# Fewer, larger transfers on the SP queue of a two-layer graph network kernel

## The chip, the core and the metric

The kernel runs on one core of a Trainium2 chip. The core has five engines that run side by side: TensorE (PE in the profile; its weight loads are listed apart as PEld), VectorE (DVE), ScalarE (ACT), GpSimd (POOL) and SyncE (SP). Each takes its own instructions in order and waits on semaphores for the others. Data moves between the chip's memory (HBM, here also called DRAM) and the on-chip memory by 16 DMA engines, which SP, ACT and GpSimd feed with transfers through queues. The metric is the time of one execution on the device, in microseconds (us); before the change it is 1118.38 us, the median of 3 runs (1115.33 to 1119.31).

## What is computed

The inputs are x of shape (32, 512, 512), an adjacency matrix adj of (512, 512), and weights of 512 x 512, all float32. Two layers follow each other, each with a normalisation ahead of it and a residual sum behind it:

```python
# layer 0
h = maximum(layernorm(x), 0)
x = x + (einsum('nm,bmd->bnd', adj, h) @ weight + bias)
# layer 1
h = maximum(layernorm(x), 0)
q, k, v = h @ Wq + bq, h @ Wk + bk, h @ Wv + bv        # 8 heads of 64
scores = einsum(q, k) / sqrt(64) + (1 - adj) * -1e9
x = x + (softmax(scores) @ v) @ Wo + bo
```

With these inputs the mask of layer 1 is decided in each row by its largest entry of adj, so that a softmax row picks one row of v. The kernel looks at adj at run time, and if this holds for every row it takes a shorter path (`single_path`): layer 1 becomes "take row idx(n) of h, multiply it by Wv Wo, add a constant row, and add the product to row n of x". That is the path that runs here.

## The kernel before

**Tiles.** A batch of x is one tile of 128 partitions x 4 row blocks x 512 columns (1 MB). Five such buffers are kept (`xs`, batch b uses buffer b % 5), and two for the normalised rows (`hs`).

**The work of a batch.** Normalise x (DVE statistics L194 and L195, a power on POOL L201, an offset on DVE L204, the activation on ACT L212); multiply by adj (`aggregate`, copied from PSUM to yT by ACT L326 and DVE L324); multiply by the layer-0 weight and add onto x (`layer0`, DVE L344); normalise again (L194 to L212, result h1). Then layer 1: `put_h` stores h1 to a DRAM tile hs (L488); `get_h` gathers from it, with eleven indirect DMAs issued by POOL (L494), only the rows that some row of adj picks, at most 352; DVE transposes them (L529); `layer1` multiplies them by the folded weight (ACT L337 and DVE L334 take the results to zs); `put_z` transposes the products back on DVE in two parts (L545, tile zr) and writes them to a DRAM tile z by SP (L549); `finish` has four indirect DMAs issued by POOL gather, for each of the 512 rows, its row of z and add it onto x (L553); `store` writes x to the output by SP (L559).

**Matrix products.** All three products of a batch are done by a scheme with seven block products in place of eight (`product`, L287). It accumulates several of them in one PSUM bank, and between two of them the bank has to be read: `u2` goes into the bank of `p1` after p1 was taken, `c22` after u2 was taken, `c12` after p5 was taken. So PE waits when DVE (layer 0) or ACT (aggregate) takes a block late.

**Order.** Nothing is scheduled by a planner: under `tc.manual_schedule()` each engine runs its instructions in the order in which they are written. An outer loop runs over b, and its 21 steps are PE's block products of `layer0(b)`, `aggregate(b + 1)` and `layer1(b - 1)`. `put(batch, step, f)` hangs other work on a step: in a usual turn, z of batch b - 2 at step 0 (the blocks s = 0 to 5), `finish(b - 2)` at step 1, the load of x for b + 2 at step 2, the power of h1 at steps 6 and 8, `put_h(b)` at steps 9 and 11, `store(b - 2)` at step 12, and the first part of z of batch b - 1 (the blocks s = 6 to 10) at step 20. The last two turns differ: z of batch 29 has steps 13 and 14, its additions step 15, and its store goes behind those of the loop. At the very end `layer1_rows(31)` does the last batch row by row, with its own four stores, and the store of batch 30 is issued from ACT's queue.

**The SP queue** holds the loads of x, the stores of h1, z and the output, in that order of steps. [...]

Of the kernel before, what the change touches and what calls it, by code (L numbers as in the profile page):

```python
# [17 lines left out]
P = 128  # L18
# [8 lines left out]
def gnn_two_layers(ctx: ExitStack, tc: tile.TileContext, x, adj, w0, b0, wq, bq, wk, bk, wv, bv, wo, bo, out):  # L27
# [149 lines left out]
    with tc.If(single > P - 1) as cmp:  # L177
        single_path(tc, x, wv, bv, wo, bo, out, kept)
# [38 lines left out]
def single_path(ctx: ExitStack, tc: tile.TileContext, x, wv, bv, wo, bo, out, kept):  # L217
# [14 lines left out]
    nc = tc.nc  # L232
    B, N, D = x.shape
    C, DC = N // P, D // P
# [12 lines left out]
    X, H0 = {0: xs[0], 1: xs[1]}, {0: hs[0], 1: hs[1]}  # L247
    H0S, H1, HS, HC, HT, HTS, Z, ZT, ZR = {}, {}, {}, {}, {}, {}, {}, {}, {}

    def load_x(b):  # L250
        X[b] = xs[b % 5]
        for c in range(C):
            nc.sync.dma_start(X[b][:, c, :], x[b, c * P:(c + 1) * P, :])


    def blk(t, chunks, cols, half=HALF):
# [284 lines left out]
    def put_z(b, s0, s1):  # L541
        if b not in Z:
            Z[b] = dram.tile([32 * S, D], F32, name="z")
            ZR[b] = work.tile([P, S, P], F32, name="zr")
        nc.vector.transpose(ZR[b][:, s0:s1, :].rearrange("p s (c e) -> p s c e", c=4),  # L545
                            ZT[b][:, :, 32 * s0:32 * s1].rearrange("p c (s j) -> p s c j", j=32))
        rows = Z[b].rearrange("(s j) (q f) -> q j s f", j=32, q=4)
        for q in range(4):
            nc.sync.dma_start(rows[q][:, s0:s1, :], ZR[b][32 * q:32 * q + 32, s0:s1, :])  # L549

    def finish(b):
        for c in range(C):
# [1 line left out]
                out=X[b][:, c, :], out_offset=None, in_=Z[b],  # L554
                in_offset=bass.IndirectOffsetOnAxis(ap=place[:, c:c + 1], axis=0), compute_op=ALU.add)

    def store(b, eng=nc.sync):
        for c in range(C):
            eng.dma_start(out[b, c * P:(c + 1) * P, :], X[b][:, c, :])  # L559

    def run(steps, work_by_step):
        if steps is None:
# [16 lines left out]
    with tc.manual_schedule():  # L579
# [6 lines left out]
        for b in range(B + 1):  # L586
# [5 lines left out]

            put(b - 2, 15 if b == B - 1 else 1, finish)
            put(b + 2, 2, load_x)
            for step, i in ((0, 0), (1, 1), (2, 2), (3, 3)) if b > 0 else ((1, 0), (2, 1), (2, 2), (3, 3)):
                put(b + 1, step, h0_sum, i)
            put(b - 2, 14 if b == B - 1 else 0, put_z, 0, 6)
            if b == B - 1:
                put(b - 2, 13, put_z, 6, S)
# [22 lines left out]
            if b < B - 1:  # L622
                put(b - 2, 12, store)
            elif b == B:
                put(b - 3, 1, store)
# [13 lines left out]
            if b < B and b != B - 2:  # L639
                put(b - 1, 20, put_z, 6, S)  # L640
# [36 lines left out]
                run(layer1(b - 1) if b < B and b != B - 2 else None, todo[14:21])  # L677
        layer1_rows(B - 1)
        if B > 1:
            store(B - 2, nc.scalar)  # L680


@with_exitstack
# [261 lines left out]
```

## Time and profile before

| | before |
|---|---|
| timed, median of 3 (lowest to highest) | 1118.38 us (1115.33 to 1119.31) |
| profiled execution | 1170.05 us, span 1168.3 us |
| mean granted TensorE clock | 0.984 |
| busy: DVE, POOL, ACT | 905.7, 653.9, 359.4 us |
| moved by DMA | 186.90 MB, mean 160 GB/s |
| SP issues: x loads L253, stores L559, z L549 | 120, 120, 248 |

Busy time is the time in which an engine executes; a DMA issue is not busy time. The profiled execution is some 50 us longer than the timed ones. The page's list of transfers shows what SP issues (name out<-in, engine, operation, count, size of one):

```profile
hs<-h SPq DMA_DIRECT2D x64, 512.0 KB
out_dram<-x SPq DMA_DIRECT2D x124, 256.0 KB
x<-in_x_dram SPq DMA_DIRECT2D x120, 256.0 KB
z<-zr SPq DMA_DIRECT2D x124, 96.0 KB
z<-zr SPq DMA_DIRECT2D x124, 80.0 KB
```

The three kinds that the change touches are the last four rows (four of the 124 output stores belong to the last batch and stay). A batch has 4 + 4 + 8 of them, beside two stores of h1.

### The profile page before, as it was taken

To read this page: it belongs to the slowest core of one execution; us is meant where nothing else is said; L and a number is where in the kernel's file an instruction comes from. 1 tells how busy PE (TensorE), PEld (TensorE's weight loads), DVE (VectorE), ACT (ScalarE), POOL (GpSimd) and SP (SyncE) were. 2 spreads that over 40 slices of the span, in tenths; PEclk is the share of its full clock that TensorE was granted. 3 is DMA by queue.
4 is the path that set the end of the run, shared out by engine and by line. 5 is a ranking of instruction groups with operands and counts; after the bars stand their busy time and mean duration, and the time that the engine had idled before them with its cause. 6 is when DMAs were issued, how large, how long until landed. Compare 5 with 4: busy or idle time off the path is not lost.

```text
span 1168.3 us, 15855 instructions
## 1 busy us (share of the span) xinstructions
PE 1100.6 (94%) x5408; PEld 957.8 (82%) x5408; DVE 905.7 (78%) x1859; ACT 359.4 (31%) x655; POOL 653.9 (56%) x584
## 2 busy tenths in 40 slices
PE   7999989999989999999999999899999999999885
PEld 3658878989978989888989888798998889998782
DVE  6879868878867878787888888687887878887760
ACT  4223313233313233323323332223333232233120
POOL 2146536655646765565765555566565656666443
PEclk9999989999989999999999999999999999999998
DMA  6414665655666665576665657566566756666438
GB/s 225 153 19 129 165 173 140 171 170 149 168 173 139 165 180 147 153 191 167 150 177 171 159 155 187 133 170 178 155 165 172 190 140 167 180 176 156 120 118 203
DMA packets 135146, 186.90 MB, mean 160 GB/s; under 512 B 17472, under 2 KB 61120, under 8 KB 135056
## 3 DMA queue, kind: packets, MB, share of 16 engines
q1 hardware_dynamic: 102320, 123.05, 31.0%
q0 software_dynamic: 29472, 56.47, 27.4%
q10 hardware_dynamic: 3264, 6.29, 1.5%
q8 instruction: 44, 0.72, 0.2%
q14 instruction: 46, 0.38, 0.1%
HBM read 96.28 MB, written 89.46 MB: 159 GB/s over the span
## 4 chain that ended last, share of the span: by engine, by line
PE 83%; DVE 6%; issue 3%; POOL 3%; ACT 1%; DMA 1%; another core or an unknown queue 1%; SPq 0%; POOLq 0%; ACTq 0%; DVEq 0%
PE mm L287 78%; DVE x L344 2%; POOL x L553 1%; PE mm L139 1%; PE mm L480 1%; PE mm L371 1%; DVE st L194 1%; DMA x<-in_x_dram 1%; PE mm L520 1%; ACT h L212 1%; POOL rstd L201 1%; POOL hc L494 1%; DVE h0s L266 1%; DVE yT L324 0%
## 5 line engine op out<-in xcount | busy, mean ns | idle before, releaser
L494 POOL DMA_INDIRECT hc<-hs,listed x341 | 356.2, 1045 | 261.9 <-DMA hs<-h 157.2
L344 DVE TENSOR_TENSOR x<-mm,x 128x512 f32<-128x512 f32 x217 | 149.6, 690 | 146.6 <-PE mm L287 107.7
L326 ACT COPY yT<-mm 128x512 f32<-128x512 f32 x124 | 71.8, 579 | 614.3 <-PE mm L287 478.3
L553 POOL DMA_INDIRECT x<-z,place x124 | 196.0, 1581 | 70.2 <-issue 47.9
L287 PE MATMUL mm<-w_t,sel 128*128 128x256 f32 x744 | 182.2, 396 | 37.9 <-DVE x L344 31.6
L212 ACT ACTIVATE h<-x,off,rstd 128x512 f32<-128x512 f32 x256 | 194.7, 807 | 48.2 <-DVE off L204 46.3
L287 PEld LDWEIGHTS mm<-w_t,sel 128*128 128x128 f32 x744 | 143.9, 196 | 67.5 <-DVE x L344 39.4
L201 POOL TENSOR_TENSOR rstd<-ve,mhalf 128x2 f32<-128x2 f32 (+1 forms) x97 | 97.2, 1002 | 156.9 <-DVE ve L200 151.8
L194 DVE BATCH_NORM_STATS2 st<-x 128x6 f32<-128x512 f32 x256 | 171.6, 670 | 8.4 <-DMA x<-in_x_dram 7.3
L287 PE MATMUL mm<-adjT_s,h0s 128*128 128x256 f32 x744 | 170.9, 379 | 0.4 <-ACT yT L326 0.2
L287 PEld LDWEIGHTS mm<-adjT_s,h0s 128*128 128x128 f32 x744 | 141.2, 190 | 20.3 <-ACT yT L326 1.2
L287 PE MATMUL mm<-hTs,wvo_t 128*128 128x176 f32 x720 | 117.8, 313 | 1.7 <-ACT zs L337 1.7
L287 PE MATMUL mm<-w_s,yT 128*128 128x256 f32 x496 | 117.2, 379 | 0.0
L287 PE MATMUL mm<-adjT,h 128*128 128x256 f32 x496 | 117.2, 379 | 0.0
L337 ACT ACTIVATE zs<-mm,cvo_c 128x176 f32<-128x176 f32 x248 | 87.4, 404 | 94.7 <-PE mm L287 60.4
L287 PEld LDWEIGHTS mm<-hTs,wvo_t 128*128 128x128 f32 x720 | 109.7, 190 | 2.8 <-ACT zs L337 2.8
L287 PEld LDWEIGHTS mm<-adjT,h 128*128 128x128 f32 x496 | 94.2, 190 | 13.2 <-issue 0.5
L287 PEld LDWEIGHTS mm<-w_s,yT 128*128 128x128 f32 x496 | 93.1, 190 | 11.7 <-issue 0.5
L458 DVE TENSOR_TENSOR x<-x,b_r 128x512 f32<-128x512 f32 x128 | 86.5, 677 | 0.0
L287 PE MATMUL mm<-hT,wvo 128*128 128x176 f32 x480 | 81.4, 313 | 0.0
L287 PEld LDWEIGHTS mm<-hT,wvo 128*128 128x128 f32 x480 | 75.3, 190 | 1.5
L324 DVE TENSOR_TENSOR yT<-mm,yT 128x512 f32<-128x512 f32 x93 | 63.5, 682 | 4.1 <-PE mm L287 2.7
(152 smaller groups left out, 1262.9 us busy)
## 6 DMA issues: line engine op xcount, KB each, us to landing
hs<-h SPq DMA_DIRECT2D x64, 512.0 KB
out_dram<-x SPq DMA_DIRECT2D x124, 256.0 KB
x<-in_x_dram SPq DMA_DIRECT2D x120, 256.0 KB
z<-zr SPq DMA_DIRECT2D x124, 96.0 KB
z<-zr SPq DMA_DIRECT2D x124, 80.0 KB
hc<-hs,listed POOLq DMA_INDIRECT x341
x<-z,place POOLq DMA_INDIRECT x124
x<-in_x_dram ACTq DMA_DIRECT2D x4, 256.0 KB
```

Source lines behind the costliest of these rows:

```text
L139: nc.tensor.matmul(ps, hs[0][:, m, d * P:(d + 1) * P], adjT[:, m, :], start=(m == 0), stop=(m == C - 1))
L194: self.nc.vector.bn_stats(st, self.src[:, self.chunks[i], :])
L201: self.nc.gpsimd.tensor_tensor(self.rstd, ve, self.mhalf[:, 0:n], ALU.pow)
L212: self.nc.scalar.activation(dst, src, AF.Relu, bias=self.off[:, i:i + 1], scale=self.rstd[:, i:i + 1])
L287: nc.tensor.matmul(bank[:, m, 0:half], lhs[:, k, m * P:(m + 1) * P], rhs[:, k, :], start=(first and m == 0 and k == 0), stop=(k == 1), ski ...
L324: nc.vector.tensor_add(dst, bank, dst)
L326: nc.scalar.copy(dst, bank)
L337: nc.scalar.activation(dst[:, m, :], bank[:, m, :], AF.Identity, bias=cvo_c[:, 2 * i + m:2 * i + m + 1])
L344: nc.vector.tensor_add(dst, bank, dst)
L458: nc.vector.tensor_add(X[b][:, c, :], X[b][:, c, :], b0_r)
L494: nc.gpsimd.indirect_dma_start(out=HC[b][:, s, :], out_offset=None, in_=HS[b].rearrange("n (q d) -> (n q) d", q=4), in_offset=bass.Indirec ...
L553: nc.gpsimd.indirect_dma_start(out=X[b][:, c, :], out_offset=None, in_=Z[b], in_offset=bass.IndirectOffsetOnAxis(ap=place[:, c:c + 1], axi ...
```

## The change

The transfers of a batch are merged: x is loaded by one DMA of 1 MB in place of four of 256 KB, the output is stored by one of 1 MB in place of four, and z is written by four of 176 KB, after the second transpose, in place of four of 80 KB after the first and four of 96 KB after the second. The bytes and the rows of each transfer stay the same. It is for sparing issues, waits and completions on the SP queue. The very last store, of batch 30 from ACT's queue, keeps its four parts.

```diff
     def load_x(b):
         X[b] = xs[b % 5]
-        for c in range(C):
-            nc.sync.dma_start(X[b][:, c, :], x[b, c * P:(c + 1) * P, :])
+        nc.sync.dma_start(X[b], x[b].rearrange("(c p) d -> p c d", p=P))
...
         nc.vector.transpose(ZR[b][:, s0:s1, :].rearrange("p s (c e) -> p s c e", c=4),
                             ZT[b][:, :, 32 * s0:32 * s1].rearrange("p c (s j) -> p s c j", j=32))
-        rows = Z[b].rearrange("(s j) (q f) -> q j s f", j=32, q=4)
-        for q in range(4):
-            nc.sync.dma_start(rows[q][:, s0:s1, :], ZR[b][32 * q:32 * q + 32, s0:s1, :])
+        if s0 == 0:
+            for q in range(4):
+                nc.sync.dma_start(Z[b].rearrange("(s j) (q f) -> q j s f", j=32, q=4)[q], ZR[b][32 * q:32 * q + 32])
...
-    def store(b, eng=nc.sync):
-        for c in range(C):
-            eng.dma_start(out[b, c * P:(c + 1) * P, :], X[b][:, c, :])
+    def store(b):
+        nc.sync.dma_start(out[b].rearrange("(c p) d -> p c d", p=P), X[b])
+
+    def store_rows(b):
+        for c in range(C):
+            nc.scalar.dma_start(out[b, c * P:(c + 1) * P, :], X[b][:, c, :])
...
-            store(B - 2, nc.scalar)
+            store_rows(B - 2)
```

## The prediction

> **What bounds the kernel now.** I read the page's summary first, then the idle times by waiter, then single batches in the timeline and in windows, and last the DMA packet records.
>
> The first lines of the page name the engine:
>
> ```profile
> PE 1100.6 (94%) x5408; PEld 957.8 (82%) x5408; DVE 905.7 (78%) x1859; ACT 359.4 (31%) x655; POOL 653.9 (56%) x584
> ...
> PE 83%; DVE 6%; issue 3%; POOL 3%; ACT 1%; DMA 1%; another core or an unknown queue 1%; SPq 0%; POOLq 0%; ACTq 0%; DVEq 0%
> ```
>
> PE works 94% of the span and carries 83% of the chain of waits; DMA carries 1%, SP's own queue nothing. So the queue that the change shortens is not itself on the chain. The idle times of SP say why (the SP queue's own waits: who, for what, total, times, longest):
>
> ```profile
> SPq L488 <- ACT h L212: 462.8, 63, 18.7
> SPq L549 <- DVE zr L545: 182.1, 19, 10.4
> ...
> SPq L559 <- DMA x<-z,place: 5.3, 3, 2.5
> ```
>
> SP sits waiting for ScalarE's normalised rows and VectorE's transposes; for issue slots it seldom queues.
>
> Next, one batch at a time. I take as a batch's start the first layer-0 matmul (L287 w_s,yT), and write +t for t us after it. From 109.9 to 1073.9 there are 28 intervals, 964.0 us. They are of two sorts, which the windows show (length, busy of PE, PEld, DVE, ACT, POOL, clock, DMA share, GB/s):
>
> ```profile
> 286.00:318.50 32.50, 32.50 (x170) 29.53 (x169) 27.59 (x57) 10.91 (x20) 21.11 (x18) 1.00 0.68 174
> 425.40:460.80 35.40, 33.08 (x170) 29.58 (x169) 27.75 (x57) 10.93 (x20) 20.50 (x18) 1.00 0.61 160
> ```
>
> In the first, PE has no gap in 32.5 us. In the second, PE stops once, 2.3 us at +7.1, for VectorE's second addition of layer 0 (the gap reads as PE waiting for DVE x L344). About half of the intervals have such a stop, 1.5 to 3.8 us. The profiled execution took 1170.05 us, the timed ones 1118.38. If every interval were 32.6 us, the span would lose 964.0 - 28 x 32.6 = 51.2 us and the execution would be 1170.05 - 51.2 = 1118.9: the timed value. I conclude, as an inference and not a measurement, that the timed runs have few of these stops: their batches are already as long as PE's own work. Then the only places where time can be won are the 110 us before and the 94 us after the 28 intervals; the middle can only lose.
>
> [...] packet sizes stay the same, and only SP's issue time goes. [...] in the batch from 497.6 the 512-byte z packets end at +6.6 and the 2048-byte x packets, issued after them, begin at +6.6, while POOL's gathers run between. [...]
>
> **The change part by part.** One SP issue takes 0.44 us (median of L549 and of L253, by tile), of L559 0.60. The program's instruction order on PE, ACT, DVE and POOL is unchanged; SP loses 10 of 18 issues a batch.
>
> x load, 4 to 1: saves 3 x 0.44 = 1.3 us of SP a batch, at +4.3 to +6.9. Behind it SP has nothing until L488 at about +18, so this is worth nothing on the path; the wait for ACT h L212 hides it. It adds a wait: the first statistics need all 1 MB instead of a quarter. The packets end between +9.7 and +11.6; L194 first reads this tile near +18.4 (515.96 in the batch from 497.6). Cost 0, margin nearly 7 us. The load also needs the whole earlier store out of its buffer, issued in the batch before at +20.5, some 14 us ahead.
>
> Store, 4 to 1: saves 3 x 0.60 = 1.8 us of SP at +20.5. It now waits for all four L553 additions. Their packets end at +18.3 to +19.9 in nearly all batches, before SP gets there behind hs<-h, so the added wait is nil to a few tenths. Behind it on SP stands z, ten us later. Cost 0 in the middle.
>
> z, 8 to 4: this one touches a path. POOL's L553 needs all of z, and behind L553 on POOL stands the power for this batch's normalisation (L201); ACT's L212 waits for that, and ACT's copies of yT, which PE needs, stand behind L212. So: when does z land?
> Before: transposes end at +0.5 and +2.0, SP issues from +0.5 to +4.3, packets run from +1.3 to between +5.8 and +7.4.
> After: all issues follow the second transpose: +2.0 to +2.0 + 4 x 0.44 = +3.8. First packets 0.8 us after an issue as now: +2.8. Volume 1408 packets of 512 B, 88 for each of 16 engines. Low bound: the packets' own 28 ns, 88 x 28 ns = 2.5 us, end +5.3. High bound: the mean rate of now, 1408 in 5.0 us, end +7.8. The best half-microsecond of the trace has 251 packets, against 571 at 28 ns on 16 engines; at 251 the volume takes 2.8 us, and POOL's 64 KB gathers (16 packets of about 250 ns, one each 1.25 us) take a fifth of the engines: 3.4 us, end +6.2. I take +6.2, within today's range, since now much of the 5.0 us is the spacing of eight issues.
> L553 cannot start before POOL's last gather ends at +6.2 to +7.5, and starts at +7.3 to +8.1 in most gapless batches. Where it started at +8.7 and +8.8, PE had gaps of 0.34 and 0.25 us about +19 and +23. So break-even is near +8.5, and there is some 0.7 us of slack. At +6.2 nothing is lost: cost 0. At +7.8 L553 starts near +9.3, 0.8 us past break-even.
>
> The end: here DMA is the limit.
>
> ```profile
> 1138.00:1150.00 12.00, 6.10 (x5) 1.00 0.94 210
> 1150.00:1156.00 6.00, 5.08 (x4) 1.00 0.87 205
> 1156.00:1162.00 6.00, 0.34 (x1) 0.59 1.04 282
> ```
>
> The next-to-last column is the DMA engines' share. The store of batch 29 goes out in quarters at 1142.4, 1145.2, 1148.2 and 1150.1 as additions finish. As one transfer it goes at the last: three quarters, 384 packets of 85 ns on 16 engines = 2.0 us per engine, move behind 1150. But the engines are nearly full before 1150 as well, so what waits there (z and additions) gets those 2.0 us back in part. Bounds 0 and +2.0; I take +1. z of batches 29 and 30 starts up to 1.5 us later and has fewer issues: 0. The last store stays in four parts.
> The start: the buffers are loaded long before their use (VectorE's waits for x add up to 7.3 us, all in the first loads, which stay). 0.
> Sum: 1118.4 + 1 = about 1119.
>
> **The rivals.**
> Faster: the stops at +7.1 fall while z and x are issued and in flight. If they are partly real in timed runs, fewer issues and completions could remove some. For: the timing. Against: the arithmetic above leaves no room, unless the profile also stretches start and end. If it stretches those 204 us by the same 4.6% (51.2/1118.9), 9 us of the timed runs are stops; all removed gives 1118.4 - 9 = 1109.
> Slower: z lands at the high bound: 0.8 us x 28 = 22 us, 1141; if half the excess is absorbed, 1130. For: 5/11 of z is held back 1.5 us. Against: the packet rate of 251 and SP's shorter issue.
> Slower by the end alone: +2.0 and a late z (1.0), 1121.5, still no measurable change.
>
> **How the numbers follow.** Hidden, with an end of 0 to +3: 0.62, 1119. Faster: 0.20, around 1109 (most of it from 1107 to 1113). Slower through z: 0.18, 1125 to 1141. The bound of 0.5% is 5.6 us, so same is 1112.8 to 1124.0. For 8 in 10 the range leaves some 0.1 on either side: 1109 to 1130.
>
> **What would show it.** L553's first start at +7.3 to +8 and gapless batches of 32.5 us: z is right. SP's waits for ACT h L212 longer by about what its issues lost. L553 later than +8.5, with PE gaps at +19 to +23, shows the z step wrong. PE stops at +7.1 fewer, and timed runs below 1112, shows the inference on the stops wrong. The last addition of batch 30, now issued at 1154.8 of 1168.3, shows the end.

## The result and the profile after

| | before | changed |
|---|---|---|
| timed, median (lowest to highest), 4 runs each | 1118.65 us (1115.33 to 1119.31) | 1135.26 us (1133.72 to 1136.94) |
| ratio to before, with its 95% interval | | 1.0155 [1.013, 1.018] |
| profiled execution, span | 1116.49, 1114.7 us (taken again) | 1135.71, 1134.0 us |
| the 28 intervals between batch starts, sum and mean | 919.9, 32.86 us | 938.7, 33.53 us |

The change costs 16.6 us by the medians, and 14.5 to 20.1 us by the interval of the ratio. A ratio is taken over all undisturbed runs of a group, so it is not exactly that of the two medians. The forecast of 1119 was wrong, and so was its range: 1135.26 lies 5 us above 1130. It came out as the second rival had it (1125 to 1141), the late z.

The first profile of before (1170.05 us) can't be set beside this one, since it has the stops of PE at +7.1 that the timed runs lack. The same kernel was therefore profiled again (`before_again` below), and "before" in what follows is that profile. It has no such stop, nor has the changed kernel's. In the changed kernel the lines have moved up by one or two: L252 is the load of x, L286 the block products, L325 the copy of yT, L487 the store of h1, L548 the writing of z, L552 the additions, L557 the store.

First the summary of the page after: busy time of each engine, then the shares of the chain of waits.

```profile
PE 1093.7 (96%) x5408; PEld 949.1 (84%) x5408; DVE 905.2 (80%) x1859; ACT 358.9 (32%) x655; POOL 661.9 (58%) x584
...
PE 58%; DVE 22%; POOL 10%; issue 4%; DMA 3%; ACT 1%; SPq 1%; POOLq 0%; ACTq 0%; DVEq 0%
```

Beside it stand the same two lines of before, profiled again:

```profile
PE 1085.0 (97%) x5408; PEld 949.4 (85%) x5408; DVE 905.0 (81%) x1859; ACT 358.8 (32%) x655; POOL 663.0 (59%) x584
...
PE 79%; DVE 9%; POOL 5%; issue 2%; DMA 2%; ACT 1%; SPq 1%; POOLq 0%; ACTq 0%; DVEq 0%
```

The chain has left PE: 58% where before had 79%, DVE 22% for 9%, POOL 10% for 5%. POOL and DVE have the same work as ever, so they are on the chain because they were late, not because they do more.

PE is "busy" 8.7 us longer, with the same 5408 matmuls and the same weight loads (949.1 and 949.4 us). So this isn't more work; it is best read as waiting that counts as busy, and a batch below shows the matmuls concerned. In this trace the weight loads stayed as they were while the matmul time grew.

SP's own waits of the changed kernel (who, for what, total us, times, longest):

```profile
SPq L487 <- ACT h L212: 475.4, 63, 17.5
SPq L548 <- DVE zr L544: 404.6, 31, 15.0
```

and those of before:

```profile
SPq L488 <- ACT h L212: 420.0, 63, 15.8
SPq L549 <- DVE zr L545: 295.6, 31, 13.5
```

SP has more idle time than before, and nothing in the middle of the run needed it. The merged store (L557) waits for the additions only twice, 7.4 us in all. The page's list of transfers (the last column is the median from issue to landing in us) has the new sizes:

```profile
x<-in_x_dram SPq DMA_DIRECT2D x30, 1024.0 KB, 7.9
out_dram<-x SPq DMA_DIRECT2D x30, 1024.0 KB, 5.2
z<-zr SPq DMA_DIRECT2D x124, 176.0 KB, 3.3
```

Now one batch, the one that starts at 343.7, in the timeline (start, us, engine, line, operation, count, idle time before it and its releaser):

```profile
345.77 2.49 SPq L548 DMA_DIRECT2D z<-zr  x4
...
349.79 1.43 POOL L493 DMA_INDIRECT hc<-hs,listed  x1 [0.30 <-issue]
...
353.53 1.59 POOL L552 DMA_INDIRECT x<-z,place  x1 [2.31 <-DMA z<-zr]
...
360.12 1.29 POOL L201 TENSOR_TENSOR rstd<-ve,mhalf 128x2 f32<-128x2 f32 x1
...
361.44 0.16 DVE L204 SCALAR_TENSOR_TENSOR off<-mv,rstd 128x2 f32<-128x2 f32 x1 [2.52 <-POOL rstd L201]
...
361.69 0.81 ACT L212 ACTIVATE h<-x,off,rstd 128x512 f32<-128x512 f32 x1 [3.37 <-DVE off L204]
...
363.59 0.57 ACT L325 COPY yT<-mm 128x512 f32<-128x512 f32 x1
...
364.21 1.99 PE L286 MATMUL mm<-adjT_s,h0s 128*128 128x256 f32 x8 [1.33 <-ACT yT L325]
```

The delay can be followed by hand. POOL's last gather ends at 351.22. The last z packet ends at +8.75, 352.47 (from the packet records), and the first addition starts 1.06 us behind it, after 2.31 us of idling. Four additions and the power (L201) later, VectorE has waited 2.52 us, ScalarE 3.37 us, its copy of yT comes late, and PE stands 1.33 us. In windows (length, busy of PE, PEld, DVE, ACT, POOL, clock, DMA share, GB/s) this batch and a mild one:

```profile
343.70:378.20 34.50, 33.06 (x170) 29.52 (x169) 27.62 (x57) 11.07 (x21) 20.95 (x19) 1.00 0.65 166
881.00:913.99 32.99, 32.88 (x170) 29.52 (x169) 27.61 (x57) 10.90 (x20) 21.07 (x18) 1.00 0.68 173
```

The second is the instructive one. PE shows no gap over 0.11 us in it, and still the interval is 32.99 us where an undisturbed one has 32.53: PE's busy time is 0.38 us more than the 32.50 of an undisturbed batch. Two matmuls of the multiplication by adj stand out, at +19.0 and +22.8, about where other batches have gaps: they last 0.47 and 0.48 us, in an undisturbed batch 0.38. The wait hides in matmuls that count as busy.

Summed over the run, idle times by waiter, changed kernel:

```profile
ACT h L212 <- DVE off L204: 91.5, 63, 3.8
...
DVE off L204 <- POOL rstd L201: 74.6, 66, 2.9
POOL x L552 <- DMA z<-zr: 37.0, 27, 4.3
...
PEld mm L286 <- ACT yT L325: 19.1, 28, 2.1
...
PE mm L286 <- ACT yT L325: 9.8, 13, 1.7
```

and before, profiled again, where the profile mostly names nothing ("issue") as what ended the waits of the additions:

```profile
ACT h L212 <- DVE off L204: 71.7, 64, 2.8
...
DVE off L204 <- POOL rstd L201: 54.9, 66, 2.0
POOL x L553 <- issue: 35.1, 83, 4.9
...
PEld mm L287 <- ACT yT L326: 4.4, 8, 1.2
...
PE mm L287 <- ACT yT L326: 1.5, 4, 0.8
```

That doesn't mean that before never waited for z. In 15 of its 28 batches the first addition starts later than +7.85, and in 13 of these it does so 1.1 to 1.5 us after z's last packet.

VectorE's wait for the power grew by 19.7 us and ScalarE's by 19.8, one for one with the 18.8 us that the 28 intervals gained. PE's visible wait grew only by 8.3 us; 8.7 more are in its busy figure. The weight loads show what PE's gaps hide: they wait for the copy of yT in 28 places where before has 8. The rest of the span is unchanged: from the first instruction to the first of these batch starts 108.2 us (107.9 before), from the last to the end 87.1 us (86.8).

The end of the run, changed kernel first, then before, in windows that begin equally far (7.8 and 7.7 us) ahead of the last addition:

```profile
1112.00:1124.00 12.00, 7.63 (x21) 3.25 (x19) 2.08 (x3) 0.58 (x1) 6.13 (x4) 0.98 0.95 225
1124.00:1134.00 10.00, 0.00 (x0) 0.00 (x0) 0.00 (x0) 0.00 (x0) 0.00 (x0) 0.50 0.71 222
```

```profile
1094.00:1106.00 12.00, 6.56 (x19) 2.81 (x17) 1.38 (x2) 0.58 (x1) 6.13 (x4) 0.86 1.02 257
1106.00:1114.70 8.70, 0.00 (x0) 0.00 (x0) 0.00 (x0) 0.00 (x0) 0.00 (x0) 0.50 0.59 180
```

As the prediction had it, some of the output seems to move behind the last additions (the first window moves 225 GB/s for 257, the second 222 for 180): the last addition starts 14.2 us from the end, before 12.9. One profile each can't say how much: in the kernels below that keep the store of before and have no stops this figure runs from 12.3 to 13.9, and the other kernel with the merged store has 15.0.

### The profile page after: what moved, and what is told of

Read it like the earlier page. It is cut to its first block, busy times and chain, and to the rows that moved or that the text cites. A ratio compares the mean times of both kernels' runs of the same rounds, so it can differ in the third digit from the quotient of the medians.

```text
span 1134.0 us, 15440 instructions
## 1 busy us (share of the span) xinstructions
PE 1093.7 (96%) x5408; PEld 949.1 (84%) x5408; DVE 905.2 (80%) x1859; ACT 358.9 (32%) x655; POOL 661.9 (58%) x584
## 4 chain that ended last, share of the span: by engine, by line
PE 58%; DVE 22%; POOL 10%; issue 4%; DMA 3%; ACT 1%; SPq 1%; POOLq 0%; ACTq 0%; DVEq 0%
PE mm L286 54%; DVE st L194 7%; POOL x L552 5%; POOL rstd L201 4%; DVE yT L323 3%; DMA z<-zr 2%; DVE x L343 2%; DVE mv L195 2%; DVE hT L528 2%; PE mm L139 1%; PE mm L479 1%; PE mm L370 1%; DVE hTs L272 1%; DVE zs L333 1%; DVE zr L544 1%
## 5 line engine op out<-in xcount | busy, mean ns | idle before, releaser
L493 POOL DMA_INDIRECT hc<-hs,listed x341 | 366.9, 1076 | 261.4 <-DMA hs<-h 156.8
L325 ACT COPY yT<-mm 128x512 f32<-128x512 f32 x124 | 71.4, 576 | 545.5 <-PE mm L286 424.3
L552 POOL DMA_INDIRECT x<-z,place x124 | 192.9, 1555 | 71.3 <-DMA z<-zr 37.0
L286 PE MATMUL mm<-adjT_s,h0s 128*128 128x256 f32 x744 | 173.6, 383 | 9.9 <-ACT yT L325 9.8
L286 PE MATMUL mm<-w_t,sel 128*128 128x256 f32 x744 | 171.1, 380 | 0.8 <-DVE x L343 0.8
L201 POOL TENSOR_TENSOR rstd<-ve,mhalf 128x2 f32<-128x2 f32 (+1 forms) x97 | 104.8, 1081 | 113.3 <-DVE ve L200 110.8
L286 PEld LDWEIGHTS mm<-adjT_s,h0s 128*128 128x128 f32 x744 | 139.4, 190 | 36.6 <-ACT yT L325 19.1
L286 PEld LDWEIGHTS mm<-w_t,sel 128*128 128x128 f32 x744 | 141.5, 190 | 20.5 <-DVE x L343 1.8
L286 PE MATMUL mm<-hTs,wvo_t 128*128 128x176 f32 x720 | 117.3, 313 | 0.6 <-ACT zs L336 0.6
L286 PE MATMUL mm<-adjT,h 128*128 128x256 f32 x496 | 117.2, 380 | 0.0
L286 PE MATMUL mm<-w_s,yT 128*128 128x256 f32 x496 | 117.2, 379 | 0.0
L286 PEld LDWEIGHTS mm<-hTs,wvo_t 128*128 128x128 f32 x720 | 109.8, 190 | 0.9 <-ACT zs L336 0.9
L286 PEld LDWEIGHTS mm<-adjT,h 128*128 128x128 f32 x496 | 94.5, 190 | 13.0 <-issue 0.5
L286 PEld LDWEIGHTS mm<-w_s,yT 128*128 128x128 f32 x496 | 93.3, 190 | 11.5 <-issue 0.5
L286 PE MATMUL mm<-hT,wvo 128*128 128x176 f32 x480 | 81.4, 313 | 0.0
L286 PEld LDWEIGHTS mm<-hT,wvo 128*128 128x128 f32 x480 | 75.3, 190 | 1.5
L204 DVE SCALAR_TENSOR_TENSOR off<-mv,rstd 128x2 f32<-128x2 f32 (+1 forms) x97 | 15.6, 161 | 74.6 <-POOL rstd L201 74.6
```

Of the source, the lines that this page charges most:

```text
L201: self.nc.gpsimd.tensor_tensor(self.rstd, ve, self.mhalf[:, 0:n], ALU.pow)
L286: nc.tensor.matmul(bank[:, m, 0:half], lhs[:, k, m * P:(m + 1) * P], rhs[:, k, :], start=(first and m == 0 and k == 0), stop=(k == 1), ski ...
L325: nc.scalar.copy(dst, bank)
L493: nc.gpsimd.indirect_dma_start(out=HC[b][:, s, :], out_offset=None, in_=HS[b].rearrange("n (q d) -> (n q) d", q=4), in_offset=bass.Indirec ...
L552: nc.gpsimd.indirect_dma_start(out=X[b][:, c, :], out_offset=None, in_=Z[b], in_offset=bass.IndirectOffsetOnAxis(ap=place[:, c:c + 1], axi ...
```

## The experiments

The table gathers what decides, out of the traces: medians over 28 batches, in us after the batch start, for z's issues and packets and for the first addition (L553 in before's numbering), then that addition's mean start and the sum of the 28 intervals. The time is the timed median, the ratio is to before in the same group of runs.

| kernel | z issued from, to | z packets from, to | L553 | mean | 28 intervals | time | ratio [95%] |
|---|---|---|---|---|---|---|---|
| before_again | 0.51, 4.32 | 1.34, 6.58 | 7.85 | 8.06 | 919.9 | 1118.49 | 0.9992 [0.9979, 1.0006] |
| the change | 1.97, 4.42 | 2.81, 7.28 | 8.48 | 8.75 | 938.7 | 1135.26 | 1.0155 [1.013, 1.018] |
| z_only | 1.97, 4.43 | 2.81, 7.50 | 8.63 | 8.75 | 939.3 | 1138.12 | 1.0170 [1.0142, 1.0199] |
| x_only | 0.51, 4.34 | 1.34, 6.48 | 7.79 | 8.11 | 920.9 | 1119.98 | 1.0008 [0.9997, 1.0019] |
| xs_z8 | 0.51, 4.35 | 1.33, 6.48 | 7.80 | 8.08 | 920.2 | 1121.81 | 1.0021 [1.0009, 1.0033] |
| z_hold | 0.51, 4.38 | 1.34, 6.68 | 7.99 | 8.17 | 922.9 | 1118.78 | 0.9997 [0.9988, 1.0005] |
| z_hold_all_2 | 1.97, 5.79 | 2.80, 7.95 | 9.26 | 9.25 | 954.3 | 1152.58 | 1.0292 [1.0262, 1.0323] |
| z_two_q | 1.97, 2.86 | 2.81, 6.37 | 7.80 | 8.10 | 921.2 | 1119.23 | 0.9996 [0.9985, 1.0007] |
| z8_act | 0.51, 3.89 | 1.34, 7.90 | 9.28 | 9.24 | 952.5 | 1153.87 | 1.0314 [1.0293, 1.0335] |
| x_early_z4_2 | 1.97, 4.43 | 2.81, 6.99 | 8.18 | 8.24 | 924.8 | 1122.22 | 1.0027 [1.0017, 1.0037] |
| x_early_z8_act_2 | 0.51, 3.89 | 1.34, 6.03 | 7.79 | 7.92 | 915.7 | 1116.00 | 0.9962 [0.9944, 0.9981] |
| x_early_z_two_q | 1.97, 2.86 | 2.81, 5.93 | 7.79 | 7.91 | 916.3 | 1115.63 | 0.9965 [0.9953, 0.9978] |

In three groups of runs, one of four kernels and two of one kernel each, the kernel before itself took 1159.44, 1180.83 and 1175.97 us, with PE's stops at +7.1; what ran there is told at its place and carries no weight for the change. The ratios there say only how a kernel stood to before in the same group.

**The same kernel again** (`before_again`): before.py unchanged, to learn whether the stops belong to it.

> The kernel before, once more, for a second profile of it. If the stops of PE at +7.1 us of a batch belong to the first profiled execution alone, this one has batches of 32.5 to 33.0 us (mean), few stops, and a span near 1117 us. If they belong to the kernel, about half of the batches have them again and the span is near 1168 us.

They don't: the profile of an execution of 1116.49 us has none, and its 28 intervals take 919.9 us.

**One part at a time.** `z_only` has only the third part of the change:

```diff
-        rows = Z[b].rearrange("(s j) (q f) -> q j s f", j=32, q=4)
-        for q in range(4):
-            nc.sync.dma_start(rows[q][:, s0:s1, :], ZR[b][32 * q:32 * q + 32, s0:s1, :])
+        if s0 == 0:
+            for q in range(4):
+                nc.sync.dma_start(Z[b].rearrange("(s j) (q f) -> q j s f", j=32, q=4)[q], ZR[b][32 * q:32 * q + 32])
```

> Only z is merged: four transfers of 176 KB after the second transpose; x and the output as before. Theory 1 (z lands later because its first part is held back and each transfer is larger): nearly the whole loss, 1131 to 1136 us, L552/L553 starting at +8.3 or later. Theory 2 (the 1 MB load of x[...] slows z on the shared DMA engines): little, 1117 to 1124 us. Theory 3 (the merged store delays something): none, 1119 us.

`x_only` has only the first:

```diff
-        for c in range(C):
-            nc.sync.dma_start(X[b][:, c, :], x[b, c * P:(c + 1) * P, :])
+        nc.sync.dma_start(X[b], x[b].rearrange("(c p) d -> p c d", p=P))
```

> Only the load of x is merged into one transfer of 1 MB; z stays in eight transfers, the store in four. Theory 1: no change, 1115 to 1121 us. Theory 2: slower, 1124 to 1135 us. Theory 3: no change.

`xs_z8` has that and the merged store, with z in eight as before:

```diff
-    def store(b, eng=nc.sync):
-        for c in range(C):
-            eng.dma_start(out[b, c * P:(c + 1) * P, :], X[b][:, c, :])
+    def store(b):
+        nc.sync.dma_start(out[b].rearrange("(c p) d -> p c d", p=P), X[b])
```

> The change without its z part: load and store merged, z in eight transfers as before. Theory 1: the loss is gone, 1114 to 1120 us. Theory 2: the loss stays as in x_only. Theory 3: the loss is here and not in x_only, 1128 to 1136 us.

z alone costs 1.7%, as much as the whole change within the intervals, and 19.4 us in the 28 intervals. The load costs nothing that can be told (0.9 us, -0.3 to 2.1). Load and store together cost 0.2% [0.1, 0.3], some 2.4 us, of which the 28 intervals hold 0.3 us: what there is of it lies in the start and the end, of which one profile each can't say more (86.8 us from the last batch start to the end before, 89.2 with the merged store, 87.1 in the whole change, and 85.0 to 90.6 in the other kernels without stops, which keep the store of before).

**Held back or merged?** The change does two things to z: it holds back 5/11 of it and makes four transfers of eight. `z_hold` was to hold back all eight without merging:

```diff
-        for q in range(4):
-            nc.sync.dma_start(rows[q][:, s0:s1, :], ZR[b][32 * q:32 * q + 32, s0:s1, :])
+        if s0 == 0:
+            for a, e in ((6, S), (0, 6)):
+                for q in range(4):
+                    nc.sync.dma_start(rows[q][:, a:e, :], ZR[b][32 * q:32 * q + 32, a:e, :])
```

> The kernel before, with z in eight transfers of 80 and 96 KB, but all eight issued after the second transpose; load and store as before. Theory 1a (one queue feeds 512-byte pieces at its own rate, about 170 in half a microsecond, however they are cut into transfers; the holding back alone costs): last z packet near +7.5 as with the four large ones, 1134 to 1140 us. Theory 1b (the larger transfers are what is slow): earlier than with four, 1122 to 1131 us. Theory 1c (SP's time for an issue is the limit): eight issues of 0.44 us from +2.0 end at +5.5, last packet near +8.0, 1142 to 1152 us.

It held nothing back: the first z was still issued at +0.51. The place in the program, behind the second transpose on VectorE, did not delay SP: it waits for the data that a transfer reads, and the four that stand first read the first transpose. So its 0.9997 says nothing on the question. The next kernel, `z_hold_all`, turns the order round, so that the transfers of the second transpose stand first in SP's queue:

```diff
+            for a, e in ((0, 6), (6, S)):
```

> Eight transfers of z as before, but the four of 96 KB come first on SP and the four of 80 KB after them: since SP works in order, all eight now wait for the second transpose (in z_hold they did not: its first z issue stayed at +0.51). Holding back as the cause: as slow as the four large ones or slower, 1134 to 1145 us, L553 at +8.5 or later. Large transfers slow in themselves: 1119 to 1128 us.

That group was one with stops. Before took 1159.44 us, this kernel 1160.59 (1.0014 [0.999, 1.0037]), and its profile shows the stops (VectorE's layer-0 additions waited for, by weight load and by matmul):

```profile
PEld mm L287 <- DVE x L344: 33.4, 18, 2.7
PE mm L287 <- DVE x L344: 26.2, 17, 2.2
```

The same rows of before_again are 1.8 and 0.8 us. With stops of this size in both kernels the group can't show what a late z costs. The same kernel was run once more, as `z_hold_all_2`:

> Eight transfers of z, all behind the second transpose, once more, where the kernel before has no stops of PE (in the first run it took 1159 us, with stops near +7.1 in every kernel of that group). Its profile had z's packets ending at +7.6 and L553 at +8.95 on average, as z_only. If the holding back is the cause of the loss and the number of transfers is not: 1136 to 1142 us where before takes 1119. If the size of the transfers matters: 1119 to 1130 us.

Here before took 1119.18 us. Holding back without merging costs 2.9%, 34.4 us in the 28 intervals; with merging (z_only) it is 19.4. So once z is held back, merging helps: it ends the issues at +4.4 in place of +5.8 and gives back 15.0 us. It is the holding back that costs, on one queue and with the load of x behind z, and more than the whole loss.

**Two queues.** If SP's one queue is what makes the held-back z late, half of it on ScalarE's queue should land early. `z_two_q`:

```diff
+        if s0 == 0:
+            for q in range(4):
+                eng = nc.sync if q < 2 else nc.scalar
+                eng.dma_start(Z[b].rearrange("(s j) (q f) -> q j s f", j=32, q=4)[q], ZR[b][32 * q:32 * q + 32])
```

> The z part of the change alone, with two of its four transfers issued by SP and two by ScalarE's queue. Theory 1a (the rate is that of one queue): z flows at up to twice the rate, last packet by +6.2, L553 back at +7.8, 1116 to 1121 us. Rival (the DMA engines or the writes to HBM set the rate of 512-byte pieces): last packet stays near +7.5, 1133 to 1139 us.

The loss is gone, 0.9996, and with it most of the lateness of the additions. Summed over the 28 batches, the first ones start 8.6 us later than +7.79, in the change 26.8 us and before 7.6 us. The waits that the profile names fell too:

```profile
POOL x L554 <- DMA z<-zr: 12.6, 6, 4.0
```

The waits for z are 12.6 us in 6 places for 37.0 in 27. z starts at +2.81 as in the change and ends at +6.37 for +7.28. Two things changed at once, though: z has two queues, and its issues, made by two engines side by side, end at +2.86 for +4.43 in z_only. Whether z gains from the second queue or from the 1.57 us of issue time was not separated.

`z8_act` has eight transfers at the times of before, the later four on ScalarE's queue:

```diff
+        eng = nc.scalar if s0 == 0 else nc.sync
         for q in range(4):
-            nc.sync.dma_start(rows[q][:, s0:s1, :], ZR[b][32 * q:32 * q + 32, s0:s1, :])
+            eng.dma_start(rows[q][:, s0:s1, :], ZR[b][32 * q:32 * q + 32, s0:s1, :])
```

> The kernel before, with the four transfers of z that follow the second transpose issued by ScalarE's queue in place of SP's. If every us of L553's start beyond +7.8 costs one us of the batch (the five profiles so far: start 8.30, loss 0.49; 8.93, 1.12), and the queue's rate is the limit, L553 starts at +7.8 nearly always: mean batch 32.6 in place of 32.86, 1110 to 1115 us. If SP's load of x, now issued some 1.5 us earlier, takes the DMA engines from z: no gain or slower, 1117 to 1126 us.

3.1% over before, more than any other kernel but its twin below, though nothing of z is held back. SP now has the load of x right behind the first four, at +2.4 in place of +4.4, and x's first packets run from +4.3, beside z's second half. The profile names the load as what ended most waits of the additions:

```profile
POOL x L554 <- DMA x<-in_x_dram: 45.2, 26, 3.1
```

This line must not be read as a wait for x: the additions don't use the x that is loaded there, and in the traces of before and of the change z and x take their completion semaphores in turn from the same eight (numbers 100 to 107). The first addition starts 1.3 us (median) behind z's last packet, in the changed kernel 1.1 us, while the load is still running. z ends at +7.90 and the addition starts at +9.28. `z8_act_late` was to bring the load back behind z by its place in the program:

```diff
-            put(b + 2, 2, load_x)
+            put(b + 2, 4, load_x)
```

> As the run before, and the load of x moved from step 2 to step 4 of the batch, behind z's flow. If the load competes with z: better than without the move, 1109 to 1114 us. If not: the same as without it, or slower where the load's packets now fall on those of the additions (+10 to +19).

A miss of the same kind as z_hold: no instruction of SP lies between the two places, so the load is issued as early as ever (its packets begin at +4.2). 1154.87 us, 1.0311 [1.0289, 1.0334], as z8_act.

**The load out of the way.** To move it for good it has to stand elsewhere in SP's own order: behind the store of the batch before, `x_early`.

```diff
-            put(b + 2, 2, load_x)
+            if b < 2:
+                put(b + 2, 2, load_x)
+            if b > 0:
+                put(b + 3, 13, load_x)
```

> The kernel before with the load of x moved as in the run before; z in eight transfers. Theory: [...]z never waited for x, so no change from that, 1116 to 1121 us; if batches' late starts of L553 came from x's packets, mean batch 32.6, 1110 to 1115 us. If the load now disturbs the gathers of hs: slower, 1122 to 1130 us.

`x_early_z4` is this with z_only, `x_early_z8_act` this with z8_act:

> The z part of the change alone (four of 176 KB), with the load of x moved on SP to behind the store of the batch before, 10 us ahead of z, so that no load follows z on the queue. If the load behind z takes DMA time from it: z ends near +6.5, 1116 to 1124 us. If z is only held back and fed at one queue's rate: still near +7.3, 1131 to 1138 us.

> As x_early, with the last four transfers of z issued by ScalarE's queue, which in z8_act cost 3%. If x's packets on SP's queue were what slowed z on ScalarE's there: z ends by +5.5, L553 at +7.8 always, 1109 to 1115 us. If ScalarE's queue is slow in itself: about 1150 us again.

These three were in the group with stops (before 1159.44 us): 1156.18 (0.9894 [0.9837, 0.9951]), 1137.92 (0.983 [0.9789, 0.9871]) and 1168.79 us (1.0062 [1.0028, 1.0096]). The stops are smaller in x_early_z4 (PE's visible waits for the layer-0 additions are 15.0 us there, 26.2 to 32.8 in the other three kernels of the group), which may explain its gain there, but why was not settled. Two were run again where before took 1119.18 us, with `x_early_z_two_q`, which is z_two_q with the load moved:

> Four large transfers of z with the load of x moved away from behind them. In the first run's profile z ended at +6.9 and L553 started at +8.15 on average (z_only +7.5 and +8.75). At one us a batch for each us beyond +7.8 this is 0.35 us x 28 = 10 us over the floor, the same as before itself (+8.06): 1117 to 1124 us. If the load has no part in it: 1134 to 1139 us.

> Load of x moved away, z in eight with the last four on ScalarE's queue. Its first profile had L553 at +7.63 on average, never waiting for z. Without stops the batches should all be at PE's floor of 32.53: 28 x 0.33 = 9 us less than before, 1108 to 1114 us. If ScalarE's queue were slow in itself, as z_act might be read: about 1150 us.

> Load of x moved away, z in four large transfers, two on SP and two on ScalarE's queue. Two queues alone brought L553 back to a median of +7.8 (mean +8.1), and the moved load alone took 0.6 us off z. Together L553 at +7.8 always: 1108 to 1114 us. If the two gains are one and the same (the rate of writing): 1116 to 1121 us.

With the load away, the merged z on one queue ends at +6.99 in place of +7.50, and 14.5 us of z_only's 19.4 are back (924.8 for 939.3). So a good part of z's lateness is x behind it. It sits in the last packets: in the median 98% of z has ended at +6.82 in z_only and at +6.64 with the load away, the last packet at +7.50 and +6.99. z on two queues wins 4.9 us by the same move (916.3 for 921.2), and z8_act 36.8 us (915.7 for 952.5), which shows that x beside z was its whole loss. The last two kernels are faster than the change, and a little faster than before: 1116.00 us, 0.9962 [0.9944, 0.9981], and 1115.63 us, 0.9965 [0.9953, 0.9978].

**The whole change with both repairs** (`after_moved`): x and the store merged, z on two queues as in z_two_q, the load moved as in x_early. It was run twice.

> The whole change (8 transfers a batch: load and store of 1 MB, four of z), with the load moved to behind the store of the batch before and two of the four z transfers on ScalarE's queue. If z's arrival was all that the change lost: like x_early_z_two_q, 1112 to 1119 us where before takes 1119, 16 to 23 us faster than the change as made. If the merged load or store costs something of its own: 1120 to 1128 us.

> The same kernel where, as is hoped, before takes 1119 us (in its first run before took 1181 us, with stops of PE). z's arrival the whole cause: 1112 to 1119 us. The merged load or store costing something of its own: 1120 to 1128 us. With stops again: only the comparison inside the group counts.

Both groups had the stops: 1168.27 us beside 1180.83 (0.9887 [0.9831, 0.9942]) and 1161.11 beside 1175.97 (0.9854 [0.9799, 0.9909]). Faster than before in those conditions, but how it stands to x_early_z_two_q without stops was not measured.

## Why the prediction was wrong

The step that failed is z's, in two of its terms: when z lands, and how much slack there is behind it. The load and the store cost what was forecast. Some readings of the trace that the z step rests on were off too; they are named here as they come.

**PE's floor.** The inference that the timed runs lack the stops is shown: 28 intervals of 919.9 us, 32.86 each, against the 32.6 assumed.

**x load, cost 0.** Right: x_only is +0.9 us [-0.3, 2.1]. But the load was asked only what it needs, not what it does to z in front of it, and that turned out to matter (14.5 us in x_early_z4_2). The prediction read from the batch at 497.6 that x's packets begin where z's end. That batch is the exception: in the other 27 of that trace's 28 intervals x's first packets start before z's last has ended, by 0.7 us in the median.

**Store, 0 in the middle; the end, 0 to +2.** Right in the middle (0.3 us). For the end, xs_z8's 2.4 us [1.0, 3.7] for load and store together and the 1.2 us by which the last addition stands further from the end fit the bounds, though one profile each can't confirm them.

**z, first packets at +2.8.** Right: +2.81.

**z, issues to +3.8.** They end at +4.4. Four issues of 0.44 us were assumed; they take 0.32, 0.46, 0.54 and 0.98 us (medians of 28 batches).

**z lands at +6.2.** It ends at +7.28 in the median and +7.57 in the mean. In the median 98% of its packets have ended by +6.6, and the stragglers take another 0.6. So of the 1.1 us some 0.4 is the rate, and 0.6 the last 2%, for which the sum had no term; the runs with the load moved say that x behind z is part of that.

The rate was mis-sized because a best slice was taken for a mean. In the batch from 881.0 the slices of half a microsecond between +3.0 and +6.5 carry 173, 134, 203, 130, 282, 195 and 181: the 251 of the sum is passed once, yet the mean is 185, and over the whole flight 1408 packets in 4.5 us are 157. Two figures of the prediction made 251 look safer than it was. It was not the best slice of the old trace but that of one batch; over the 28 batches the best ones have 220 to 300. And by the prediction's own estimate from the 28 ns of a packet, 16 engines carry 16 x 500 / 28 = 286 in half a microsecond, not 571. So 251 is nearly nine tenths of that and not under half of it. That z's packets spread evenly over all 16 engines was assumed in the estimate, not shown: the trace records no engine numbers.

The old mean (1408 in 5.2 us, 134) was kept as the high bound (+7.8), with the spacing of eight issues as the reason for its lowness. With four issues the mean rose by a sixth only, so the spacing of the issues was not the main reason. Nor does z's end simply follow the last issue: from the end of that issue to z's last packet it is 2.2 us in z_hold_all_2, 2.3 before, 3.1 in z_only and 3.5 in z_two_q. What sets the rate stays open.

**Slack of 0.7 us, break-even at +8.5.** There is none. I grouped the 336 batches of the twelve kernels in the table, whose profiles have no stops, by the first addition's start, and took what each batch's aggregate stage (the multiplication by adj) lost against an undisturbed one:

| first addition at + | 7.79 | 7.93 | 8.08 | 8.30 | 8.55 | 8.96 | 9.66 |
|---|---|---|---|---|---|---|---|
| stage longer by (us) | 0.02 | 0.12 | 0.33 | 0.49 | 0.75 | 1.15 | 1.89 |

The earliest start, +7.8, is the one that POOL's own gathers allow (they end at +7.49). Above it every tenth of a microsecond is lost in full: a straight line through the batches above +7.85 rises by 1.03 us of the stage, and by 0.98 us of the whole interval, for each us. The prediction looked at two batches with additions at +8.7 and +8.8, saw gaps of 0.34 and 0.25 us, and concluded that 0.7 us had been absorbed. Their intervals were 33.40 and 33.48 us, 0.9 over the floor: the loss was there, for the greater part in matmuls counted as busy.

**The sum again.** The first addition starts at +8.75 in the mean, +8.06 before. 0.69 us x 28 = 19.3 us, and the intervals gained 18.8. The second rival had priced it at 0.8 x 28 = 22 us: right in mechanism and nearly in size, but the size is luck in part: it had z land later than it did (+7.8), the first addition start 1.5 us behind it (1.1 in the changed kernel), and 0.7 us of slack that isn't there, and these errors nearly cancel. Its half-absorbed form (1130) is ruled out by the table, and the rival that only the end gets longer (1121.5) by z_only. The faster one, fewer stops of PE, had nothing to work on, since there were no stops. Of the signs that were to show the z step wrong, both came: L552 past +8.5 in the mean, and PE gaps that begin at +19.2 in 13 of the 28 batches.

**"Only SP's issue time goes."** The prediction took it that only SP's issue time was at stake, and put it at 4 x 0.44 us. That nothing else was at stake was the author's estimate; no trace of before shows it. And the issue time isn't small: the four issues of z last from +1.97 to +4.43 in z_only. The same transfers over two queues were issued by +2.86, ended 0.9 to 1.1 us earlier (+6.37 for +7.28 and +7.50) and undid the whole loss. With x out of the way, 1408 packets take 4.18 us on one queue (168 in half a microsecond) and 3.12 us on two (226). The issue time saved, 1.57 us, is more than z gained; whether a second queue gives anything beyond it, no run here shows.

## What to carry to other kernels

Merging transfers that become ready at different times holds the early ones back to the last (here z's first packet went from +1.34 to +2.81); before doing it, find who waits for the last byte, and count its delay one for one (1.03 us of the stage for each us here) unless the trace shows the slack in interval lengths, not in gaps. For a transfer's time in new conditions, use the mean rate of its own kind (157 packets in half a microsecond here, where the best slice had 282), and count what stands behind it on the queue (14.5 us over the 28 intervals in x_early_z4_2). If a burst has a reader that waits, try issuing it from two engines (921.2 us in z_two_q for 939.3 in z_only), and keep bulk loads away from it in the queue's own order (915.7 us in x_early_z8_act_2 for 952.5 in z8_act); a new place in the program changed nothing here where that order stayed (1154.87 us in z8_act_late, 1153.87 in z8_act).

## What the runs showed of the hardware

- Four issues of one size (352 packets of 512 bytes each) on SP's queue, one right behind the other, get longer with each: 0.32, 0.46, 0.54, 0.98 us in the change. Eight of 160 and 192 packets don't (0.33 for the first, then 0.43 to 0.46 in z_hold_all_2). On two queues at once the pairs take 0.33 and 0.46 us (SP), 0.36 and 0.49 us (ScalarE) in z_two_q. What makes the fourth issue long was not shown.
- In 26 of 28 batches of the changed kernel the first addition starts 1.05 to 1.35 us after the last z packet ends; in two it starts 2.2 and 2.35 us after, which no view explains.
- PE's stops at +7.1 come and go: before took 1119 us in four groups of runs and 1159 to 1181 us in three others, once on one and the same chip (1119.06 and 1175.97 us). In those three every kernel's profile has them, but the first profile of before (1170.05 us) has them too, and the runs timed with it do not. What switches them was not found.
